# Lead of the projections and place of the x gathers in a sparse graph attention with residual layer norm

## The chip, the cores and the metric

The kernel runs on one core of one Trainium2 chip. The metric is the device time of one execution in microseconds. The chip runs the work on separate engines, each with its own queue of instructions: PE multiplies matrices, DVE does vector arithmetic, ACT computes activations and copies, POOL (GpSimd) issues the indirect DMAs and does a few small operations, and SP issues most of the plain DMAs.

## The reference

For 16 batches of 1024 nodes with 512 features, eight heads of 64:

```python
q = (x @ Wq + bq).reshape(b, n, H, HD)
k = (x @ Wk + bk).reshape(b, n, H, HD)
v = (x @ Wv + bv).reshape(b, n, H, HD)
scores = einsum('bqhd,bkhd->bhqk', q, k) / sqrt(HD)
scores = scores + (1.0 - adj)[None, None, :, :] * -1000000000.0
attn = softmax(scores, axis=-1)
out = einsum('bhqk,bkhd->bqhd', attn, v).reshape(b, n, d)
x = layernorm(x + out @ Wo + bo)
```

One adjacency matrix serves all batches. It is sparse, and the first rows have far more neighbours than the last ones: an edge between nodes i and j has a probability that falls with the square roots of both.

## The kernel before, in words

The kernel does not multiply with the full adjacency. It sorts the 1024 queries by their number of neighbours, cuts them into eight tiles of 128 (t = 0 to 7), and looks up for each query the list of its keys. All further work goes by *blocks*: a block (b, t, i) takes, for the 128 queries of tile t in batch b, one key per query. Own blocks take the i-th key of each query of the tile; deep blocks (BLOCKS, tiles 6 and 7) take further keys of the queries that have many, and a matmul with a 0/1 matrix (`sums`) adds their results to the right queries. The list of all blocks has 530 entries, 32 or 34 a batch, and `start[b]` is the first of batch b: 430 for batch 13, 464 for 14, 496 for 15.

For one block, POOL gathers 128 rows of keys and values (`kvg`, L1242) from DRAM, DVE multiplies them with the queries (`qk`, L1263) and sums by head (`s`, L1267), ACT takes the exponential (L1278), ACT or DVE weighs the values (`pv`, L1291 and L1295), and DVE adds them (L1307) or PE adds them for deep blocks (L1316, L1317). At a tile's end DVE divides by the sum (`o`, L1337), PE transposes the result (`poT`, L1351), ACT copies it (`oT`), and `finish` has PE multiply it with Wo (`po`, L790). `complete` then adds the residual x and normalises: DVE (L1099, L1100), ACT (squares, L1107), POOL (the power, L1113 and L1143), ACT (L1121) and a POOL scatter to the output (L1125).

Before its blocks a batch needs its projections. These are the *fronts*: a list of PE units for all batches in order. For a pair of tiles they hold the transposition of x (`pxT`, L748), the products for q (`pq`, L790), and seven products that give k and v of two tiles by a Strassen scheme (`x`, `pp`, `z`, L947). The results of each are written to DRAM (`q_rows`, `kv_pair`) by SP, and the blocks gather from there. Two batches from batch 2 on form a pair: they share a table `kv_pair`, tile 0 of the even batch is served in the odd one, and at an odd batch's start POOL also gathers `more` (L1217) from the pair's table.

The order of everything is written by a loop over places n = -39 to 541, one place for each block, at build time. At place n the program issues the kvg gather of block n + 8 (n + 11 when the fronts have run out), the products and scores of block n + 4, the exponential of n + 3, the weighting of n + 1 or n + 2, the addition of n, and the delayed steps that earlier places planned: `later(k, fn)` runs fn k places later. PE's place in this order goes by credit: each place adds a `share` of PE time, and units of the fronts or of finishing tiles are issued until the credit is used up. The planner counts 0.86 us for a product, 0.44 for a transposition and 0.87 for a sum. At each batch's start the share is set so that the fronts still to come meet a goal:

```python
ahead = EARLY + FIRST * (1 - max(0, b - 1) / LATE)
goal = fronts_time - needed(b + 2, ahead / NBT)
```

`ahead` is thus the lead in places: how much of batch b + 2 is to be done when batch b ends. From batch 13 on (LATE + 1) the share is set so that the fronts run out at `fronts_end`. When fronts and tiles compete, a finished tile waits in `done`; some tiles (`SPILL`, 20 of them) are stored to DRAM meanwhile and are reloaded and finished only after the fronts have run out, up to one a second place.

x comes in tiles of 128 rows into three buffers. `load_x(b, t)` takes a buffer and, from batch 1 on, has POOL gather the rows (L1001). It is called from `out`, the step one place behind the transposition of an earlier tile, for the tile three further on: there ACT copies the transposed tile (`xT`), for tile 0 it also squares the rows of x (`sq_x`, L762), and for tiles in `STORED` SP writes x to DRAM (`residual`, L764), to be read again as the residual. A gather into a buffer waits until what still reads that buffer has finished; the buffers are given out in the order of the calls, the one released first first.

Of the kernel before, what the change touches and what calls it, by code (L numbers as in the profile page):

```python
# [38 lines left out]
PAIRED_FROM, SPARED = 2, 56  # L39
# [9 lines left out]
AHEAD_LAST = 11  # L49

ROWS = 3
EARLY = 13

FIRST = 11
LEAD_IN = 39
FRONT_BY = -14
SEGMENT = 64
# [120 lines left out]
def kernel(  # L178
# [37 lines left out]
    B, N, D = x.shape  # L216
    HD = D // HEADS
    NPAIR = D // P
    NT = N // P
# [34 lines left out]
    with ExitStack() as main:  # L254
# [6 lines left out]
        def fill_psum(name):  # L261
            return psum.tile([P, HALF], F32, tag="fill", name=name, bufs=4)
# [74 lines left out]
        def merged(b):  # L337
            return b >= PAIRED_FROM and b % 2 == 1
# [103 lines left out]
        def later(k, fn):  # L442
            plan.setdefault(now[0] + k, []).append(fn)
# [288 lines left out]
        def load_x(b, t):  # L732
            if b < B:
                if b and not known:
                    waiting.append((b, t))
                    return
                X[b, t] = work.tile([P, D], F32, tag="x", name=f"x_{b}_{t}", bufs=3)
                if b:
                    gather_x(X[b, t], b, t)
                else:  # L740
                    nc.sync.dma_start(X[b, t], x[b, ds(t * P, P), :])

        def transpose_x(b, t):
            def pe():
                xs = X.pop((b, t))
                p = fill_psum(f"pxT_{b}_{t}")
                for c in range(NPAIR):
                    nc.tensor.transpose(p[:, ts(c, P)], xs[:, ts(c, P)], ident)  # L748

                def out():  # L750
                    XT[b, t] = work.tile([P, D], F32, tag="xT", name=f"xT_{b}_{t}", bufs=4)
                    nc.scalar.copy(XT[b, t], p)
                    n = b * NT + t + 3
                    if t == 0 and b >= PAIRED_FROM:
                        if not merged(b):
                            BOTH[b // 2] = work.tile([P, 2, NPAIR, P], F32, tag="place", name=f"both_{b}", bufs=1)
                        nc.scalar.copy(
                            BOTH[b // 2].rearrange("p w c (h n) -> p h c w n", h=2)[:, b % 2],
                            p.rearrange("p (c w n) -> p c w n", c=NPAIR, w=2),
                        )  # L760
                        sq = work.tile([P, D], F32, tag="ysq", name=f"sq_x_{b}", bufs=1)
                        nc.scalar.activation(sq[0:LONE, :], xs[0:LONE, :], AF.Square, accum_out=x_norm[0:LONE, b:b + 1])  # L762
                    if b * NT + t in STORED:
                        nc.sync.dma_start(residual[b * NT + t], xs)  # L764
                        later(2, lambda: load_x(n // NT, n % NT))
                    else:
                        load_x(n // NT, n % NT)
                    if t % 2 and (b, t) != (0, 1):
                        later(1, combine)

                def combine():
                    s = [work.tile([P, HD2], F32, tag=f"s{i}", name=f"s{i}_{b}_{t}", bufs=1 + i // 4) for i in (1, 2, 3, 4)]
                    x0, x1 = XT[b, t - 1], XT[b, t]
                    nc.vector.tensor_tensor(s[0], x1[:, 0:HD2], x1[:, HD2:D], op=OP.add)
                    nc.vector.tensor_tensor(s[2], x0[:, 0:HD2], x1[:, 0:HD2], op=OP.subtract)
                    nc.vector.tensor_tensor(s[1], s[0], x0[:, 0:HD2], op=OP.subtract)
                    nc.vector.tensor_tensor(s[3], x0[:, HD2:D], s[1], op=OP.subtract)
                    SX[b, t // 2] = s

                later(1, out)  # L780

            return [(TRANSPOSE, pe, lambda: (b, t) in X)]
# [217 lines left out]
        def gather_x(y, b, t):  # L1000
            nc.gpsimd.indirect_dma_start(  # L1001
                out=y, out_offset=None, in_=x_rows,
                in_offset=bass.IndirectOffsetOnAxis(ap=asked_row[:, t:t + 1], axis=0), element_offset=b * N * D,
            )
# [181 lines left out]
        start = [min(n for n, block in enumerate(blocks) if block[0] == b) for b in range(B)] + [len(blocks)]  # L1186
# [276 lines left out]
        with tc.manual_schedule():  # L1463
# [9 lines left out]
            def needed(b, part):  # L1473
                b += int(part)
                if b >= B:
                    return fronts_time
                return fronts_by[b - 1] + (part - int(part)) * (fronts_by[b] - fronts_by[b - 1])

            finishing, last_finish, reloads, last_reload = [], -LEAD_IN, 0, 0
            fronts_end = start[B - 1] - 12  # L1480
            credit = 0.0
            for t in range(3):
                load_x(0, t)
            n = -LEAD_IN
            while n < total or plan or rest or urgent or done or finishing or spilled or lone_tiles or not guarded:
# [6 lines left out]
                elif n in start:  # L1492

                    b = start.index(n)
                    left = sum(u[0] for u in fronts)
                    ahead = EARLY + FIRST * (1 - max(0, b - 1) / LATE)
                    goal = fronts_time - needed(b + 2, ahead / NBT)
# [107 lines left out]
```

## Time and profile before

| what | us |
|---|---|
| median of 3 runs | 1888.14 |
| lowest and highest | 1887.98, 1894.98 |
| the profiled execution | 1894.52 |
| its span in the profile | 1892.4 |

The profile is of one execution, and its span leaves 2.1 us of that execution's time outside. The prediction shows lines of several of its views. A line of the page's groups or of the timeline names the source line, the engine, the operation and the tiles, written `out<-in` without buffer numbers. The chain of waits goes back from the last instruction to what released it, and lists start, length, engine, tile and line; `issue` is time in which the engine waited for nothing that the profile shows. A line of the waits names who waited for whom, the total, the number of times and the longest. In the busy times by window, each engine has its busy microseconds and, in brackets, its instructions. Records of PE overlap, so that their mean duration is longer than their distance in a stream.

### The profile page before, as it was taken

The page shows a single profiled execution, that of the slowest core. Times are in us where ns is not written, and L with a number is a line of the kernel's source. Part 1 is how long each engine was busy: PE and PEld are TensorE (multiplying, and loading weights), DVE is VectorE, ACT ScalarE, POOL GpSimd, SP SyncE. Part 2 cuts the span into 40 slices and gives each one's busy share as a digit, 9 for nine tenths or more (in the row PEclk, how much of TensorE's full clock was granted, in tenths as well). Part 3 has the DMA queues.
Part 4 walks back from the last instruction along what each step waited for, and adds up shares of the span by engine and source line. Part 5 has one row for each costly group of instructions (what it writes and reads, how often), then busy time and mean ns, then how long its engine had stood idle before and what let it go on. Part 6 is the DMA issues. An engine that isn't in the chain of part 4 may idle for free. (4 is left out here: it accounts for less than half of the span.)

```text
span 1892.4 us, 25171 instructions
## 1 busy us (share of the span) xinstructions
PE 1816.5 (96%) x5149; PEld 876.6 (46%) x5149; DVE 1695.3 (90%) x3470; ACT 1557.4 (82%) x6128; POOL 1262.6 (67%) x1189
## 2 busy tenths in 40 slices
PE   7979999999999999999999999999999999999996
PEld 3434444444545454444444444444545444444442
DVE  6888879999998999899999989899999989997875
ACT  3627868988888988988898878988899989977885
POOL 1366765777676776767676766767676866656884
PEclk9989999999999999999999999999999999999998
DMA  7356786888989897989889897989889899989993
GB/s 279 115 167 215 226 290 229 309 298 291 322 266 319 303 333 256 345 290 310 299 284 329 279 324 261 334 303 309 286 302 352 297 332 319 329 282 319 340 332 137
DMA packets 188149, 544.63 MB, mean 288 GB/s; under 512 B 32602, under 2 KB 32622, under 8 KB 187986
## 3 DMA queue, kind: packets, MB, share of 16 engines
q0 software_dynamic: 116400, 382.82, 60.4%
q1 hardware_dynamic: 68510, 154.30, 21.7%
q10 hardware_dynamic: 3076, 5.82, 0.8%
q14 instruction: 120, 0.98, 0.2%
q8 instruction: 43, 0.70, 0.2%
HBM read 419.52 MB, written 144.34 MB: 298 GB/s over the span
## 5 line engine op out<-in xcount | busy, mean ns | idle before, releaser
L1291 ACT ACTIVATE pv<-kvg,pv 128x64 f32<-128x64 f32 x3544 | 893.4, 340 | 1.8 <-issue 1.8
L1242 POOL DMA_INDIRECT kvg<-kv_pair,place_row x462 | 522.6, 1131 | 258.6 <-issue 94.5
L790 PE MATMUL po<-wo,oT 128*128 128x512 f32 x816 | 379.2, 600 | 2.0 <-DVE vsum L854 1.2
L790 PE MATMUL pq<-wq,xT 128*128 128x512 f32 x792 | 369.4, 598 | 1.3 <-DVE s L1267 0.8
L1267 DVE TENSOR_REDUCE s<-qk 128x8 f32<-128x512 f32 x530 | 360.8, 681 | 7.2
L1263 DVE TENSOR_TENSOR qk<-qt,kvg 128x512 f32<-128x512 f32 x434 | 296.8, 684 | 13.2 <-DMA kvg<-kv_pair,place_row 13.1
L947 PE MATMUL x<-b,xT 128*128 128x512 f32 x504 | 239.0, 597 | 0.1
L947 PE MATMUL pp<-t,s 128*128 128x512 f32 x504 | 237.3, 593 | 1.5 <-DVE t L383 1.5
L1307 DVE TENSOR_TENSOR pv<-pv,pv 128x520 f32<-128x520 f32 x329 | 228.4, 694 | 8.2 <-ACT pv L1291 8.0
L790 PEld LDWEIGHTS po<-wo,oT 128*128 128x128 f32 x816 | 153.4, 192 | 171.7 <-issue 162.7
L790 PEld LDWEIGHTS pq<-wq,xT 128*128 128x128 f32 x792 | 149.0, 192 | 169.3 <-issue 157.7
L1001 POOL DMA_INDIRECT x<-in_x_dram,asked_row x120 | 129.6, 1080 | 103.5 <-PE pxT L748 35.4
L1278 ACT ACTIVATE pv<-s,absent 128x8 f32<-128x8 f32 x434 | 126.8, 293 | 55.1 <-DVE s L1267 36.6
L1125 POOL DMA_INDIRECT out_dram<-y,asked_row x129 | 145.1, 1125 | 35.9 <-issue 25.0
L800 ACT ACTIVATE sq_k<-kv 128x128 bf16<-128x128 f32 x512 | 150.8, 300 | 8.4 <-DVE kv L970 4.5
L947 PEld LDWEIGHTS x<-b,xT 128*128 128x128 f32 x504 | 95.3, 192 | 111.6 <-issue 105.2
L947 PEld LDWEIGHTS pp<-t,s 128*128 128x128 f32 x504 | 94.1, 190 | 111.3 <-issue 102.2
L947 PE MATMUL z<-b,s 128*128 128x512 f32 x252 | 121.4, 604 | 13.1 <-DVE kv L975 10.4
L1196 POOL DMA_INDIRECT qg<-q_rows,query_row x96 | 105.5, 1099 | 28.5 <-issue 25.3
L1029 POOL DMA_INDIRECT y<-in_x_dram,asked_row x93 | 105.0, 1129 | 26.1 <-issue 25.8
L947 PE MATMUL z<-t,s 128*128 128x512 f32 x252 | 118.6, 593 | 0.0
L947 PE MATMUL pp<-t,xT 128*128 128x512 f32 x252 | 118.5, 592 | 0.0
(276 smaller groups left out, 2750.2 us busy)
## 6 DMA issues: line engine op xcount, KB each, us to landing
kv_pair<-kv SPq DMA_DIRECT2D x98, 512.0 KB
q_rows<-q SPq DMA_DIRECT2D x106, 256.0 KB
qt<-q_rows SPq DMA_DIRECT2D x98, 256.0 KB
residual<-x SPq DMA_DIRECT2D x36, 256.0 KB
y<-residual SPq DMA_DIRECT2D x36, 256.0 KB
kv_rows<-kv SPq DMA_DIRECT2D x15, 512.0 KB
kvg<-kv_pair,place_row POOLq DMA_INDIRECT x462
kv_pair<-kv SPq DMA_DIRECT2D x28, 256.0 KB
```

The source lines that it names most:

```text
L790: nc.tensor.matmul(p, lhs(c), w[:, c, :], start=(c == 0), stop=(c == NPAIR - 1))
L800: nc.scalar.activation(sq, s[:, ts(h, P)], AF.Square, scale=scale, accum_out=sums[:, h:h + 1])
L947: nc.tensor.matmul(R[bank], l[:, ts(c, P)], right[:, c, :], start=(first and c == 0), stop=(c == 1), skip_group_check=True,)
L1001: nc.gpsimd.indirect_dma_start(out=y, out_offset=None, in_=x_rows, in_offset=bass.IndirectOffsetOnAxis(ap=asked_row[:, t:t + 1], axis=0), ...
L1125: nc.gpsimd.indirect_dma_start(out=out_rows[b, t], out_offset=bass.IndirectOffsetOnAxis(ap=rows, axis=0), in_=y, in_offset=None, element_o ...
L1196: nc.gpsimd.indirect_dma_start(out=q, out_offset=None, in_=q_rows[b % ROWS], in_offset=bass.IndirectOffsetOnAxis(ap=rows, axis=0))
L1242: nc.gpsimd.indirect_dma_start(out=KG[n], out_offset=None, in_=rows, in_offset=bass.IndirectOffsetOnAxis(ap=(place_row if b else key_row)[ ...
L1263: nc.vector.tensor_tensor(QK[n], q, KG[n][:, 0:D], op=OP.mult)
L1267: nc.vector.tensor_reduce(S[n], QK.pop(n).rearrange("p (h d) -> p h d", d=HD), axis=AX.X, op=OP.add)
L1278: nc.scalar.activation(PV[n][:, D:], S.pop(n), AF.Exp, bias=bias)
L1291: nc.scalar.activation(pv[:, ts(h, HD)], v[:, ds(D + h * HD, HD)], AF.Copy, scale=pv[:, D + h:D + h + 1])
L1307: nc.vector.tensor_tensor(PV[b, t], PV[b, t], pv, op=OP.add)
```

## The change

Three things are changed. EARLY goes from 13 to 17 and FIRST from 11 to 7, so that `ahead` is 24 places for the first batches in both kernels and 17 in place of 13 at the end. `fronts_end` goes from 12 places ahead of the last batch's start to 16. And the x gather that `out` calls comes later in two cases: behind a tile that is stored as residual four places later in place of two, and behind tile 0 from batch 2 on, where x is squared, two places later in place of at once.

```diff
-EARLY = 13
+EARLY = 17
 
-FIRST = 11
+FIRST = 7
...
                     if b * NT + t in STORED:
                         nc.sync.dma_start(residual[b * NT + t], xs)
+                        later(4, lambda: load_x(n // NT, n % NT))
+                    elif t == 0 and b >= PAIRED_FROM:
                         later(2, lambda: load_x(n // NT, n % NT))
                     else:
                         load_x(n // NT, n % NT)
...
-            fronts_end = start[B - 1] - 12
+            fronts_end = start[B - 1] - 16
```

## The prediction

> **What bounds the kernel now.** I read the page's busy times first, then the chain of waits of the last 260 us, then busy times by stage, then the waits of single engines. First the page:
>
> ```profile
> span 1892.4 us, 25171 instructions
> PE 1816.5 (96%) x5149; PEld 876.6 (46%) x5149; DVE 1695.3 (90%) x3470; ACT 1557.4 (82%) x6128; POOL 1262.6 (67%) x1189
> ```
>
> PE leads, with DVE close behind. The chain shows what a matmul really costs:
>
> ```profile
> 1677.35 3.43 PE po L790 x8
> 1680.79 1.72 PE pq L790 x4
> ```
>
> Eight records (four matmuls, one tile's output projection) take 3.43 us end to end, 0.43 a record, where the groups' mean is 600 ns: records overlap. From 1650 to 1721 us the chain holds PE pieces alone: there PE is the bound and has no gap. Summing, over the trace, each PE record's start against 0.43 us (in proportion for shorter ones), PE has gaps of 43 us in all between 384 and 1745 us, of which 10 lie in 1018 to 1124 us and 11 in 1535 to 1636 us, and none worth naming between 1636 and 1745. Columns of the next view: window, length, then busy us of PE, PEld, DVE, ACT, POOL, the granted clock, DMA share.
>
> ```profile
> 1535.00:1636.00 101.00, 93.67 (x270) 44.76 (x269) 94.44 (x181) 89.97 (x370) 66.54 (x62) 0.98 0.90 311
> 1636.00:1745.00 109.00, 107.75 (x298) 51.52 (x297) 98.33 (x198) 90.83 (x362) 65.09 (x61) 1.00 0.90 314
> 1745.00:1826.00 81.00, 78.14 (x226) 36.72 (x225) 68.06 (x190) 65.93 (x212) 66.78 (x61) 1.00 0.92 336
> 1826.00:1859.00 33.00, 31.12 (x83) 14.89 (x82) 25.79 (x65) 23.95 (x80) 23.59 (x23) 0.95 0.86 301
> 1859.00:1892.00 33.00, 16.79 (x43) 7.63 (x41) 11.37 (x45) 14.97 (x35) 14.11 (x15) 0.83 0.26 97
> ```
>
> The reader is to see a full PE up to about 1859, then an end in which nothing is full. Batch 13 begins at 1535 us, 14 at 1636, 15 at 1745 (the 430th, 464th and 496th qk product on DVE; place n's product is issued at place n-4). The last place's product starts at 1858.5. Its end is held by PE: the chain runs through output projections of older tiles, and DVE queues behind them.
>
> ```profile
> 1858.70 3.43 PE po L790 x8
> 1862.35 1.72 PE po L790 x4
> 1864.94 1.72 PE po L790 x4
> 1866.87 1.73 PE po L790 x4
> 1869.33 0.63 DVE pv L1307
> ```
>
> The waits from 1826 us on say the same of DVE (total, times, longest):
>
> ```profile
> DVE y L1100 <- PE po L790: 9.0, 4, 4.2
> ```
>
> Last, POOL between 384 and 1640 us, where the moved gathers stand:
>
> ```profile
> POOL x L1001 <- PE pxT L748: 19.2, 10, 4.3
> POOL x L1001 <- ACT sq_x L762: 10.3, 5, 3.5
> POOL x L1001 <- DMA residual<-x: 7.9, 3, 6.0
> POOL more L1217 <- issue: 6.4, 6, 4.9
> ```
>
> **The skill beside the trace.** The Trainium skill, TensorE: Matmul & The Clock Gate, section "Back-to-back issue gap" and the steps before it, says that matmuls keep program order and that a stream of them costs its columns, since drain and fill overlap. The trace agrees: 0.43 us a record in a stream against 600 ns for one. So I count 0.43, and a PE instruction moved earlier costs its full time there unless PE had a gap. DMA: Bandwidth & Descriptors, section "Anatomy of one DMA", says that a DMA's semaphore wait is served on the issuing sequencer before dispatch. The rows above agree: POOL, not a DMA engine, sat up to 6.0 us before an x gather, with the kvg gathers of later places behind it. The forecast goes by both.
>
> **Part 1, the lead.** EARLY + FIRST is 24 in both, so the first batches keep their lead; it falls to 17 places at the end in place of 13. The fronts now end at start[B-1] - 16. I followed the planner's own credits for both kernels; its units (0.86, 0.44, 0.87 us) are the trace's (3.43 / 4, 0.44, 0.87). The front units run out at place 481, not 485. No work is added or removed but one bias matmul (0.22 us) and one DVE addition (0.6 us). So this is a move. Set beside the products, PE work changes by stage as: places 68 to 430 +6.9 us, batch 13 +0.8, batch 14 +3.5 (14 output projections in place of 11), places 496 to 520 +3.7, and behind 520 -14.6: 6 output projections in place of 10, four of 3.43 + 0.22 us.
>
> Behind 520 (1826.4 us to the end, 66 us). Nine places take 32 us, of which DVE is busy 25.8 with four y rows that go away (4 x 0.75 us). At 22.8 us DVE would be the next bound; ACT and POOL stand at 24 and 23.6 and lose four square, normalise, store and load steps as well (0.8 + 0.8 us on ACT, about 2 on POOL). I take 26 us for the nine places: -6. Then the last place: its product starts at 1858.5 and its weighted value is added at 1869.3, 10.8 us later, with DVE waits for po of 2.28 and 2.35 us between and a PE backlog until 1868. Without older projections I estimate 4.8 us (product 0.69, sum 0.68, exponential 0.3, weighting and addition 0.69 each, semaphores between): -6. The remaining 23 us from there to the end are the last tile's own and stay. Together -12, bounds -4 (ACT and POOL hold the rhythm) and -14.6.
>
> Places 496 to 520 hold PE gaps of some 2 us: +3. Batch 14 is PE's without a gap: +3.5. Places 68 to 430: +6.9 falls in part into the 31 us of gaps there, but those are mostly waits for DVE, whose load moves along; I take +4.5, bounds 0 and +6.9. Batch 13 has 11 us of gaps: +0.8 costs nothing.
>
> **What the lead frees.** At the start of batch 13 POOL stands 4.95 us before it can gather, because the pair's last rows are only being written (timeline: start, length, engine, line; in brackets the idle time before it):
>
> ```profile
> 1526.75 1.96 POOL L1217 DMA_INDIRECT more<-kv_pair,place_row  x1 [4.95 <-issue]
> 1538.72 0.69 DVE L1263 TENSOR_TENSOR qk<-qt,kvg 128x512 f32<-128x512 f32 x1 [1.47 <-DMA kvg<-kv_pair,place_row]
> 1543.34 0.69 DVE L1263 TENSOR_TENSOR qk<-qt,kvg 128x512 f32<-128x512 f32 x1 [1.53 <-DMA kvg<-kv_pair,place_row]
> ```
>
> DVE then waits 3.4 us for kvg in three rows and 2.2 us for POOL. Four places are some 12 us, over twice the wait, so it goes: -4 (0 to -5.6). What is late next there is DVE, 94 of 101 us. At the start of batch 14 DVE waits 1.57 and 0.91 us for kvg: -1.5.
>
> **Part 2, the x gathers.** No DMA is added. Of the 120 gathers those behind a kept x go from 2 to 4 places later, those behind a squared x from 0 to 2, so that x tile 3 is asked for after tile 4 and takes the other's buffer. POOL's waits for squares (10.3 us) and for residual stores (7.9 us) go, and some of the 19.2 us for pxT. POOL is 70% busy there, and its kvg waits are mostly for a buffer that ACT or DVE still reads, so little of this was on the path: I take -1 (0 to -4). SP's queue keeps its order but for what the lead moves. The price is a later x. A gather is issued about four places behind its emission, and PE is as late, so the distance is gap x 3.1 us. From batch 2 on the smallest gap was 4, three times; now fourteen are 3 or 4, and x(14,5) has 1, some 3 to 5 us. The chain shows an x landing in 3.25 us and kvg in 3.8 to 8.6 us; x(14,5) itself was used 6.6 us after issue without a stall. I price +2 there (0 to +4), and nothing for gaps of 3 (9.3 us).
>
> **Sum.** -12 + 3 + 3.5 + 4.5 - 4 - 1.5 - 1 + 2 = -5.5; the four freed DMA-heavy finishes also lighten a DMA share of 0.86 to 0.92 in the end, so I round to -6. Against the profiled execution's own 1894.52 us (span 1892.4 and 2.1 around it) that is 1888.5; the profile ran 6.4 us over the median of the runs, 1888.14, and the same saving gives 1882.
>
> **Rivals.** (a) The end is not PE's: places 520 to 529 keep their 3.2 us, because ACT, POOL and DVE hand each other the work (the chain from 1819 to 1849 us runs through these three). Then the end saves only 4 us while everything before pays its 14.9 in full and nothing is freed: +11, 1899, slower. It decides once the end saves less than the earlier stages pay, about 7 us. Against it: 19 us of the chain behind 1849 are PE's. (b) The lead removes jitter too: PE's gaps of 43 us shrink by a quarter, the added work is all absorbed: -16, 1872. For it: at 1097.8 us PE waits 4 us for a DVE that had been held up. Against: DVE is over 90% busy in most stages. (c) Work is only moved and the end's gain is paid back exactly, or the gathers come late again: 1888.
>
> **How the numbers follow.** About half a percent, 9.4 us, is what a measurement of this kernel tells from no change. Forecast 0.50 (own range 1876 to 1889), (b) 0.20, (c) 0.14, (a) 0.16. Below 1878.7: all of (b) and a third of the forecast, 0.36; above 1897.6: most of (a), 0.13; the rest 0.51. The range reaches to both rivals: 1870 to 1898.
>
> **What would show it.** After: the last place's product at about 1850 us and DVE's addition some 5 us behind it; no po of stored tiles in the chain behind it; the wait of POOL for more gone at batch 13; POOL's waits for sq_x and residual gone; batch 14 no shorter; PE idle before pxT of x(14,5) at most 4 us. It is wrong if batches 2 to 12 grow by more than 7 us, if x comes late in several places, or if the rhythm behind 520 stays at 3.2 us.

## The result, and the profile after

| | us |
|---|---|
| kernel before, median of 6 runs beside the changed one | 1895.13 |
| changed kernel, median of 6 runs (1912.83 to 1918.69) | 1916.08 |
| ratio, 95% interval | 1.0106 [1.0077, 1.0135] |
| forecast | 1882, range 1870 to 1898 |

The change makes the kernel 1.06% slower, about 20 us, where 6 us less were forecast. Three of the six runs of before are those of the table ahead of the prediction; the other three took 1895.28 to 1902.64, and against their median, 1899.99, the loss is 16 us. The page of the kernel after, first lines:

```profile
span 1913.5 us, 25168 instructions
PE 1824.0 (95%) x5150; PEld 880.2 (46%) x5150; DVE 1696.0 (89%) x3469; ACT 1557.1 (81%) x6128; POOL 1260.9 (66%) x1189
```

No engine got more to do: DVE, ACT and POOL are busy for the same time as before within 2 us, and PE's 7.5 us more are hardly work either (its instructions are the same but for one bias product), as will be seen. The time went into waiting. Where it went, the stages tell. The busy times by window of the kernel after (window, length, then busy us of PE, PEld, DVE, ACT, POOL with their instructions, granted clock, DMA share, GB/s); the windows are places 68 to 430, batch 13, batch 14, places 496 to 520, 520 to 529, and the rest:

```profile
383.90:1559.90 1176.00, 1143.34 (x3266) 556.01 (x3265) 1083.18 (x2118) 1017.83 (x4114) 800.09 (x743) 0.99 0.87 300
1559.90:1658.60 98.70, 94.48 (x269) 45.37 (x268) 95.05 (x182) 91.05 (x375) 68.54 (x61) 0.98 0.90 316
1658.60:1770.40 111.80, 111.80 (x310) 53.45 (x310) 95.04 (x199) 87.72 (x345) 66.40 (x63) 1.00 0.91 327
1770.40:1850.40 80.00, 79.27 (x228) 37.55 (x227) 70.31 (x195) 71.35 (x233) 66.13 (x58) 1.00 0.87 308
1850.40:1882.80 32.40, 26.53 (x69) 12.69 (x67) 23.48 (x62) 21.96 (x69) 24.98 (x24) 0.95 0.80 273
1882.80:1913.50 30.70, 10.97 (x21) 5.03 (x21) 10.72 (x36) 11.53 (x30) 11.24 (x12) 0.59 0.19 70
```

The first row of the kernel before, whose length was not shown ahead:

```profile
384.40:1535.20 1150.80, 1131.51 (x3245) 551.05 (x3244) 1078.77 (x2110) 1015.79 (x4106) 802.45 (x740) 1.00 0.88 304
```

Against the terms of the forecast (batch 13 and the rest of before by the same places: 1535.2, 1635.9, 1745.3, 1826.4 and 1858.5 us to the end at 1892.4):

| stage | before | after | change | forecast |
|---|---|---|---|---|
| places 68 to 430 | 1150.8 | 1176.0 | +25.2 | +4.5 (0 to +6.9) |
| batch 13 | 100.7 | 98.7 | -2.0 | -4 |
| batch 14 with its start | 109.4 | 111.8 | +2.4 | +3.5 - 1.5 |
| places 496 to 520 | 81.1 | 80.0 | -1.1 | +3 |
| places 520 to 529 | 32.1 | 32.4 | +0.3 | -6 |
| place 529 to the end | 33.9 | 30.7 | -3.2 | -6 |

With -0.5 us ahead of place 68 the column gives the 21.1 us between the spans. So two terms failed: the middle, by some 20 us, and the end, by 9. The others together are within 4 us.

**The end.** The nine places last as long as before, though PE is busy for only 26.53 us of them and DVE for 23.48. The POOL part of the timeline (start, length, engine, line; in brackets the idle time ahead of it) shows that POOL has less room than its busy time says:

```profile
1855.05 1.43 POOL L1198 DMA_INDIRECT qg<-q_rows,query_row  x1 [0.31 <-issue]
1856.79 1.01 POOL L1244 DMA_INDIRECT kvg<-kv_pair,place_row  x1 [0.30 <-DMA kvg<-kv_pair,place_row]
1858.10 1.23 POOL L1127 DMA_INDIRECT out_dram<-y,asked_row  x1 [0.30 <-ACT y L1123]
1859.63 1.02 POOL L1244 DMA_INDIRECT kvg<-kv_pair,place_row  x1 [0.30 <-issue]
1860.69 0.72 POOL L1145 TENSOR_TENSOR stats<-stats,neg_half 128x2 f32<-128x2 f32 x1
```

No two of these DMAs follow each other closer than 0.30 us. Counting with each POOL instruction the idle time behind it, where that is at most 0.35 us, fills all of the 81.1 us of places 496 to 520 before and 79.6 of the 80.0 after, at a busy share of 83% (66.13 of 80.00). In places 520 to 529 it fills 27.5 of 32.1 us before and 30.0 of 32.3 after: much, but not all. DVE waits for POOL there, as the waits from 1850 us of after say, and those of 1826.4 to 1858.5 us of before:

```profile
DVE stats L1118 <- POOL stats L1115: 4.9, 2, 4.2
```

```profile
DVE stats L1116 <- POOL stats L1113: 4.2, 1, 4.2
```

The wait of 4.2 us falls into the nine places in both kernels. The experiments below show what this says of the bound, and what not.

**The middle.** PE's work can be set apart from its waiting with the 0.43 us a record of the prediction; what a record takes longer than that counts as idle time. Before to after, the work in places 68 to 430 is 1119.8 and 1126.2 us (+6.4, close to the 6.9 that the forecast counted), PE's idle time 30.9 and 49.3 (+18.4). Most of this growth, 13 us, is in long single stalls: four of over 1.4 us before, 10.0 us together, and nine of 23.0 after. Some of the larger waits of PE and DVE there, after:

```profile
PE z L949 <- DVE kv L977: 12.3, 6, 4.3
DVE y L1101 <- ACT out_mean L1050: 5.9, 5, 2.1
DVE s L776 <- PE z L949: 5.1, 2, 3.1
PE sum L1318 <- ACT pv L1293: 3.1, 1, 3.1
```

Before:

```profile
PE z L947 <- DVE kv L975: 9.2, 4, 3.9
DVE y L1099 <- ACT out_mean L1048: 0.5, 1, 0.5
```

Before has no row of s behind z. The reader is to see that no one wait grew by 18 us. There are more of them, of PE for DVE and of DVE for PE and ACT. How one comes about is seen at place 390, in PE's and DVE's rows of the timeline of after:

```profile
1423.64 1.88 PE L949 MATMUL z<-t,s 128*128 128x512 f32 x4
1425.36 1.88 PE L949 MATMUL pp<-t,xT 128*128 128x512 f32 x4
1425.63 0.42 DVE L776 TENSOR_TENSOR s<-xT 128x256 f32<-128x256 f32 x1 [2.00 <-PE z L949]
...
1427.13 0.68 DVE L1265 TENSOR_TENSOR qk<-qt,kvg 128x512 f32<-128x512 f32 x1
...
1427.73 0.69 DVE L1309 TENSOR_TENSOR pv<-pv,pv 128x520 f32<-128x520 f32 x1
...
1430.26 0.69 DVE L977 TENSOR_TENSOR kv<-z,g 128x512 f32<-128x512 f32 x1
...
1431.01 3.67 PE L949 MATMUL z<-b,s 128*128 128x512 f32 x4 [3.77 <-DVE kv L977]
```

DVE stands 2.00 us before the next pair's sums, because PE is still reading the old sums for z (the tile `s1` has one buffer). Behind that stand some 4.6 us of DVE work, and only then comes `kv<-z,g`, which empties z's bank. PE comes to the second z of the pair with nothing in between but one unit `pp`, and stands 3.77 us. PE was late for DVE, and then DVE for PE.

And the stall costs more than its length: the four records behind it take 3.67 us, where the same four take 1.88 above. The windows ahead of the stall, of the stall and behind it have the granted clock in the third column from the right:

```profile
1420.00:1427.30 7.30, 7.13 (x16) 2.96 (x16) 3.74 (x10) 7.30 (x40) 4.50 (x5) 1.00 0.76 272
1427.30:1431.00 3.70, 0.00 (x0) 0.00 (x0) 3.67 (x8) 3.70 (x19) 2.64 (x3) 1.00 0.69 209
1431.00:1434.50 3.50, 3.49 (x5) 1.44 (x6) 3.43 (x9) 3.50 (x16) 2.39 (x3) 0.52 0.71 205
```

After 3.7 us without a matmul the clock is 0.52 for the next 3.5 us. The Trainium skill, TensorE: Matmul & The Clock Gate, section "What's actually happening", says that the array falls to half rate after an idle window of about 3.4 us and needs a busy one to come back. This stall is that long; other stalls here were shorter and had the same effect (last section), so 3.4 us of unbroken idle time are not needed. PE's busy time counts these slow records at their length, and the last record ahead of a stall at its full 0.6 us, which is why PE seems to have more to do.

### The profile page after: what moved, and what is told of

It is laid out like the page before. It is cut to its first block, busy times and chain, and to the rows that moved or that the text cites. A ratio compares the mean times of both kernels' runs of the same rounds, so it can differ in the third digit from the quotient of the medians.

```text
span 1913.5 us, 25168 instructions
## 1 busy us (share of the span) xinstructions
PE 1824.0 (95%) x5150; PEld 880.2 (46%) x5150; DVE 1696.0 (89%) x3469; ACT 1557.1 (81%) x6128; POOL 1260.9 (66%) x1189
## 3 DMA queue, kind: packets, MB, share of 16 engines
q1 hardware_dynamic: 68510, 154.30, 21.4%
## 5 line engine op out<-in xcount | busy, mean ns | idle before, releaser
L1293 ACT ACTIVATE pv<-kvg,pv 128x64 f32<-128x64 f32 x3544 | 894.0, 342 | 0.3
L1003 POOL DMA_INDIRECT x<-in_x_dram,asked_row x120 | 133.2, 1110 | 81.6 <-PE pxT L748 29.4
L1127 POOL DMA_INDIRECT out_dram<-y,asked_row x129 | 150.7, 1168 | 37.0 <-issue 23.9
```

Source lines behind the costliest of these rows:

```text
L1003: nc.gpsimd.indirect_dma_start(out=y, out_offset=None, in_=x_rows, in_offset=bass.IndirectOffsetOnAxis(ap=asked_row[:, t:t + 1], axis=0), ...
L1127: nc.gpsimd.indirect_dma_start(out=out_rows[b, t], out_offset=bass.IndirectOffsetOnAxis(ap=rows, axis=0), in_=y, in_offset=None, element_o ...
L1293: nc.scalar.activation(pv[:, ts(h, HD)], v[:, ds(D + h * HD, HD)], AF.Copy, scale=pv[:, D + h:D + h + 1])
```

## The experiments

Five theories were set against each other (in the recorded expectations TensorE is PE, VectorE is DVE and ScalarE is ACT). P: POOL sets the last batch. L: the lead costs on PE in proportion to the work that it moves into places 68 to 430. X: the later x gathers cost. J: each order of PE's work has its own stalls at single places, so that parts of the change don't add. A: ACT's queue is what is late. Ratios are to the kernel before on the same chip, with 95% intervals. Chips differ (the kernel before ran 1877 to 1911 us on those used here), so traces are compared within one chip.

### The parts alone

```diff
-EARLY = 13
+EARLY = 17
-FIRST = 11
+FIRST = 7
```

> EARLY 17 and FIRST 7 alone; the x gathers and fronts_end as before. Whole change: +20 us (ratio 1.0106). Theory L (the earlier projections push PE work into stages that DVE and ACT already fill, and the end gives nothing back): this run carries most of it, +10 to +20 us, growing between places 130 and 430. Theory X (the later x gathers, with tile 3 asked for after tile 4, are what hurts): within 3 us of the kernel before. Theory J (neither has a cost of its own; each shift of PE's place against DVE and ACT re-rolls which of them waits): any size from -10 to +20, and the parts don't add up.

```diff
-            fronts_end = start[B - 1] - 12
+            fronts_end = start[B - 1] - 16
```

> fronts_end 16 places ahead of the last batch in place of 12, alone. Nothing changes before place 430. Theory L and my forecast's tail: behind place 520 fewer output projections; if the end is PE's, -4 to -8 us; if ACT, POOL and DVE hold its rhythm (my rival a), 0 to +4 us with the time from place 520 to the end still 63 to 66 us. Theory X: 0.

The third kernel has the two later x gathers of the change's diff alone:

> The two later x gathers alone (4 places behind a kept x, 2 behind a squared x); lead and fronts_end as before. Theory X: +12 to +20 us, with PE idle ahead of pxT or of the first product of a pair. Theory L: -3 to +2 us, with POOL's waits for sq_x and residual gone. Theory J: anything from -10 to +15.

The fourth has the lead and the end of the fronts, and the x gathers as before:

> The whole change without the later x gathers. Theory L: +15 to +20 us, as the whole change. Theory X: -8 to +3 us. Theory J: not the sum of the lead alone and the end alone, by 5 us or more.

| edit | ratio |
|---|---|
| lead alone | 1.0104 [1.0073, 1.0136] |
| end of the fronts alone | 1.0025 [1.0010, 1.0041] |
| later x alone | 1.0061 [1.0032, 1.0089] |
| lead and end | 1.0097 [1.0059, 1.0135] |
| all three | 1.0106 [1.0077, 1.0135] |

The three parts alone would add to +1.9%, and together they make +1.06%: they don't add. The lead by itself makes the whole loss (+21.4 us, just above what L and J had). The end alone lost 5.1 us: its expectation had -4 to -8 if the end is PE's, and 0 to +4, with 63 to 66 us from place 520 on, if it is not; those places took 63.3 us. The later x alone lost 12.5 us, at the lower edge of X and within J. The kernel with the end alone has the same order as before up to place 430, so on one chip it is the control for the lead. Its row and that of the lead for places 68 to 430:

```profile
392.30:1549.80 1157.50, 1132.81 (x3238) 550.80 (x3243) 1078.44 (x2111) 1017.86 (x4106) 799.37 (x740) 1.00 0.88 302
```

```profile
394.80:1576.30 1181.50, 1148.14 (x3257) 556.70 (x3261) 1083.52 (x2117) 1017.19 (x4113) 799.88 (x744) 0.99 0.87 297
```

+24.0 us, of which +6.3 are PE's work (1118.0 to 1124.3 by 0.43 us a record) and +17.7 its idle time (39.0 to 56.7). Both profiles are of executions above the median of their kernel, that of the lead of the slowest of its six (1934.62 us, median 1927.20), so these sizes may be somewhat high. The lead's own stalls again bring slow records: the eight of an output projection, 3.43 us in the prediction, take 6.54 behind a stall of 3.59. Timeline of PE with the lead alone:

```profile
1430.52 6.54 PE L790 MATMUL po<-wo,oT 128*128 128x512 f32 x8 [3.59 <-issue]
```

With later x alone, PE, DVE and ACT keep their order, and yet 9.7 us are lost in these places (1157.5 to 1167.2). Two waits of PE there:

```profile
PE pxT L748 <- ACT oT L1357: 5.0, 1, 5.0
PE pxT L748 <- DMA x<-in_x_dram,asked_row: 2.1, 1, 2.1
```

x came late once, x(13,5) at place 399, for 2.1 us. In the kernel with all three parts PE waits for no x in these places, and the x part adds nothing that can be told from zero (1.0097 against 1.0106). Theory X falls for the change as a whole.

The kept x's gather was then moved alone:

```diff
                     if b * NT + t in STORED:
                         nc.sync.dma_start(residual[b * NT + t], xs)
-                        later(2, lambda: load_x(n // NT, n % NT))
+                        later(4, lambda: load_x(n // NT, n % NT))
```

> Only the kept x's part of the two gathers that go two places later: the next x behind a kept x is asked for four places after in place of two; behind a squared x it stays as before. The two parts together gave +0.61%. By the wait for x(13,5) at place 399 (2.2 us, behind a kept x) this part carries most of it: +0.3 to +0.6%. If the squares' part carries it (x gathered behind sq_x, two places later in every second batch): within 0.15%.

1.0000 [0.9990, 1.0010]: a miss. By what is left, the 0.6% of both belong to the squared x's gather, to the two together, or to the chip, for the two were run on different ones; the squared part was not run alone, so this stays open.

### How much lead

Three more leads, with EARLY + FIRST kept at 24: EARLY 15 and 16, between before and the change, and 11, less than before.

> EARLY 15, FIRST 9: half of the lead's step, nothing else. Theory L (loss in proportion to the PE work that is moved into places 68 to 430): +8 to +12 us. Theory J (each order has its own stalls between PE, DVE and ACT at single places, and they don't follow the amount): not half; from -5 to +25 us, with steps at places other than those of the whole lead.

> The kernel before with EARLY 16 and FIRST 8, one step short of the change's 17 and 7. Measured leads: 11 gave +0.92%, 13 is before, 15 +0.15%, 17 +1.04%. If the loss grows smoothly behind 15 (theory L with a threshold), 16 gives +0.4 to +0.8%, with TensorE's stalls at the places of 17 (153, 244, 388, 390), shorter. If every lead has its own order and its own stalls (theory J), it can give anything from -0.2 to +1.2%, and its stalls over 1.4 us stand at other places.

> EARLY 11, FIRST 13: a shorter lead of the late batches, two places the other way. Theory L: -8 to -12 us in places 68 to 430, less what the end then has to do. Theory J: slower as well, +3 to +20 us, since the order before is one that was free of long stalls.

| EARLY | 11 | 13 | 15 | 16 | 17 |
|---|---|---|---|---|---|
| ratio | 1.0092 | 1 | 1.0015 | 1.0094 | 1.0104 |
| interval | 1.0062 to 1.0121 | | 0.9986 to 1.0044 | 1.0077 to 1.0111 | 1.0073 to 1.0136 |

(11 and 15 ran on one chip, 16 and 17 on two others.) L as a proportion falls: 15 costs almost nothing, 16 nearly all, and less lead than before costs as much as more. The kernel with the kept x alone, at 1.0000, ran on the chip of 16 and so is its control there. Their rows for places 68 to 430:

```profile
375.70:1516.50 1140.80, 1126.27 (x3232) 549.77 (x3236) 1079.02 (x2111) 1013.28 (x4101) 800.24 (x739) 1.00 0.89 306
```

```profile
375.20:1534.00 1158.80, 1135.93 (x3250) 554.66 (x3254) 1080.56 (x2113) 1012.63 (x4100) 815.26 (x743) 0.99 0.88 303
```

Of these +18.0 us, 4.7 are PE's work and 13.3 its idle time (24.7 to 38.0). So on a second chip, too, the idle time grew by more than the work. A selection of PE's stalls (us of idle time of PE at a place, read from each trace's PE rows; values under 0.6 are left out, and every kernel has others):

| place, what waits | before | 15 | 16 | 17 (lead alone) | changed kernel |
|---|---|---|---|---|---|
| 153 z | 1.23 | 0.98 | 2.06 | 4.13 | 4.26 |
| 244 poT | | | 1.92 | 1.92 | 1.92 |
| 220, 221 z | 2.67 | 2.06 | 4.03 | 1.13 | 1.06 |
| 290 z | 3.86 | | | | |
| 324 z | | 7.72 | | | |
| 388 po | | | | 3.59 | 1.48 |
| 390, 391 z | | 1.53 | 1.42 | 3.75 | 3.77 |
| 423 z | | | 2.24 | 2.66 | 2.06 |

Two of these stalls belong to the order with their length: the one at 290 is 3.84 to 3.86 us in six kernels with the lead of before (before itself, the end alone, x alone, kept x alone, ScalarE lighter, POOL's scatters moved to SP) and in none with another lead; that at 390 is 3.74 to 3.77 in five with EARLY 17. Others keep their place but not their length: the one at 388 is 3.59 us with the lead alone, 1.48 in the changed kernel and under 0.6 in the changed order with ScalarE lighter. This is what J says. It is no proof that nothing grows with the lead: 16 and 17 share the stalls at 153, 244 and 423, and the expectation for J at 16, stalls at other places, came only in part.

### POOL in the last batch

Here the tiles finished after the fronts have run out are stored by SP, a plain DMA into a scratch tensor in place of POOL's scatter; these rows are missing from the output.

```diff
             def store():
+                if not fronts:
+                    left = dram.tile([P, D], F32, name=f"left_{b}_{t}")
+                    nc.sync.dma_start(left[0:n, :], y)
+                    del Y[b, t]
+                    return
                 nc.gpsimd.indirect_dma_start(
```

> The kernel before, but tiles that are finished after the fronts have run out are stored by SP into a scratch tensor in place of POOL's scatter (the output rows of these tiles, those of about the last two batches and the stored tiles, are left out; the bytes moved are the same). Theory P: from place 496 to 520 POOL has no idle time beyond the 0.3 us between its instructions, so POOL, not PE, sets the last batch. Then places 496 to 520 shrink from 81 us to PE's work, about 76, and the whole by 6 to 12 us. If PE holds the end (my forecast): within 3 us of the kernel before.

> The changed kernel with the same scatters taken off POOL (same rows left out). Theory P: the end at last gives back what the lead moved away: from place 520 to the end 8 to 12 us less than in the kernel before with its scatters off POOL, and 10 to 18 us less than the changed kernel as a whole. If PE or DVE's own work holds the end: from place 520 to the end the same 63 us as in the changed kernel.

Before with it: 0.9929 [0.9899, 0.9959]; the changed kernel with it: 1.0049 [1.0021, 1.0077]. Windows of before with it, places 520 to 529 and the rest:

```profile
1842.40:1870.30 27.90, 27.80 (x76) 13.62 (x77) 25.10 (x65) 22.89 (x76) 8.23 (x10) 1.00 0.73 266
1870.30:1897.80 27.50, 15.99 (x45) 7.45 (x43) 11.80 (x47) 15.41 (x37) 2.20 (x4) 0.93 0.39 139
```

The changed kernel with it:

```profile
1870.60:1897.90 27.30, 24.67 (x68) 11.72 (x67) 23.41 (x62) 21.46 (x69) 8.40 (x9) 1.00 0.67 241
1897.90:1922.70 24.80, 11.17 (x21) 5.23 (x21) 10.79 (x37) 11.56 (x30) 2.98 (x4) 0.65 0.24 87
```

Behind place 520 the time falls from 66.0 to 55.4 us before and from 63.1 to 52.1 after, 11 us in both; the nine places give 4.2 and 5.1 of that, the last place and what follows it 6.4 and 5.9. So for the nine places P holds: with POOL out of the way they are shorter, and in before PE is full there (27.80 of 27.90). That the DMA share falls too is part of the edit, so POOL's queue and its DMAs' load are not told apart. POOL is not the only holder, either: with VectorE lighter (the experiment after this one), and POOL's work as it was, the nine places of before's order take

```profile
1787.70:1816.10 28.40, 26.16 (x71) 12.50 (x72) 19.93 (x63) 19.87 (x65) 21.30 (x23) 1.00 0.94 344
```

28.4 us, where the same order with ScalarE lighter takes 32.2 on the same chip. In before the nine places thus hang on POOL and DVE, which wait for one another; in the changed kernel a lighter VectorE gives little (31.6 us). The gain that I had looked for, an end some 8 to 12 us shorter in the changed kernel, is 3.3 us even with POOL free. And for places 496 to 520 P fails: they did not become shorter (84.3 and 84.2 us), and the kernel with the end alone, where POOL with its gaps fills only 75.8 us of them, takes 81.6. The changed kernel stays 1.2% behind before when both have the free POOL (1.0049 / 0.9929): the end would not have paid for the lead.

### Lighter queues on VectorE and ScalarE

If the idle time is two nearly full queues waiting for one another, lighter queues should take it away. Each edit was made in the kernel before and in the changed one. VectorE lighter:

```diff
-            QK[n] = work.tile([P, D], F32, tag="qk", name=f"qk_{n}", bufs=2)
-            nc.vector.tensor_tensor(QK[n], q, KG[n][:, 0:D], op=OP.mult)
+            QK[n] = work.tile([P, D // 2], F32, tag="qk", name=f"qk_{n}", bufs=2)
+            nc.vector.tensor_tensor(QK[n], q[:, 0:D // 2], KG[n][:, 0:D // 2], op=OP.mult)
...
-            nc.vector.tensor_reduce(S[n], QK.pop(n).rearrange("p (h d) -> p h d", d=HD), axis=AX.X, op=OP.add)
+            nc.vector.tensor_reduce(S[n], QK.pop(n).rearrange("p (h d) -> p h d", d=HD // 2), axis=AX.X, op=OP.add)
```

> The kernel before with each place's product of query and key, and its sum into scores, made over 256 of the 512 columns (half of each is left out; nothing else moves). By the rows of s<-xT (128x256: 421 ns against 684) VectorE gives back 2 x 0.26 = 0.52 us a place, 188 us in places 68 to 430, where it was idle only 79. It is the control for a_dve. If the waits between TensorE and VectorE came of VectorE's queue being nearly full (theory J), TensorE's idle time there falls from 39 us to 10 to 25, and the whole to 0.98 to 0.99 of before. If TensorE's idle comes of its own order alone (theory L), the time stays within 0.5% of before.

> The changed kernel with the same halves left out. What tells the theories apart is its time less that of b_dve, which the full kernels have at +20 us. Theory J (with the lead, TensorE's order stands worse against VectorE's nearly full queue, and each waits for the other): with room on VectorE the excess in places 68 to 430 falls from 24 us to the 6 us of TensorE's added work, and the whole is 0 to +8 us against b_dve. Theory L (the lead costs on TensorE, whatever VectorE has to do): +16 to +24. Theory A (it is ScalarE's queue that is late): also +16 to +24, as ScalarE keeps its work.

ScalarE lighter:

```diff
-                for h in range(HEADS):
+                for h in range(0, HEADS, 2):
                     nc.scalar.activation(
-                        pv[:, ts(h, HD)], v[:, ds(D + h * HD, HD)], AF.Copy, scale=pv[:, D + h:D + h + 1]
+                        pv[:, ds(h * HD, 2 * HD)], v[:, ds(D + h * HD, 2 * HD)], AF.Copy, scale=pv[:, D + h:D + h + 1]
                     )
```

> The kernel before with ScalarE's weighing of v in four copies of 128 columns in place of eight of 64 (two heads take one weight, so the weights of every other head are left out). 1772 of its 3544 copies of 340 ns go; a wider one costs somewhat more (120 columns more in the 128x512 copies of 576 ns would be 0.04 us), so about 500 us of ScalarE's 1557 go. It is the control for a_act. ScalarE was no bound of before: theory J with VectorE as the partner expects 0.99 to 1.00 of before; theory A 0.98 to 0.99, with TensorE's idle time in places 68 to 430 down from 39 us by more than 10.

> The changed kernel with the same. Against b_act, theory A (ScalarE's queue is what turns the shifted order into waits) expects 0 to +8 us, with the excess of places 68 to 430 down from 24 to about 6; theory J with VectorE as the partner, and theory L, +14 to +24.

Both at once:

> The kernel before with both lightenings at once: VectorE's products of query and key over half of the columns, ScalarE's weighing in four copies of 128 columns in place of eight of 64 (half of the products and every other head's weights are left out). The control for a_both. If TensorE's idle time in places 68 to 430 (38.9 us on one chip in the full kernel, 11.7 with VectorE alone lightened) is waits on the two engines' queues, under 6 us are left, and the whole is 0.97 to 0.985 of before.

> The changed kernel with both. Its excess over b_both in places 68 to 430 was 24 us full, 17 with VectorE lightened (7 of work, 10 of idle time), 20 with ScalarE lightened. Theory J (the two queues together turn the shifted order into waits): the idle part falls to 0 to 4 us, so that 7 to 11 us are left there, all TensorE's added work, and the whole is +5 to +12 us against b_both. Theory L (the idle part comes of TensorE's order alone): 16 to 18 us stay there, 10 of them idle, and the whole stays at +13 to +17.

Ratios to the kernel before, and places 68 to 430 in us. All six lighter kernels ran on one chip. The first row is the kernel before and the changed one; the second, for these places only, the end alone and the lead alone, both on another chip (their whole times do not compare, as they differ in the end too):

| pair | before's order | changed order | difference of medians | length | PE work | PE idle |
|---|---|---|---|---|---|---|
| full, before and changed | 1 | 1.0106 [1.0077, 1.0135] | 20.9 | +25.2 | +6.4 | 30.9 to 49.3 |
| full, end alone and lead alone | | | | +24.0 | +6.3 | 39.0 to 56.7 |
| ScalarE lighter | 0.9978 [0.9971, 0.9985] | 1.0076 [1.0056, 1.0096] | 16.7 | +20.6 | +7.1 | 19.6 to 32.6 |
| VectorE lighter | 0.9871 [0.9854, 0.9887] | 0.9945 [0.9928, 0.9961] | 14.2 | +17.7 | +7.0 | 11.7 to 22.0 |
| both | 0.9824 [0.9802, 0.9846] | 0.9904 [0.9886, 0.9922] | 15.6 | +15.3 | +7.9 | 8.9 to 16.0 |

Lighter queues do take PE's idle time away: on this one chip it falls in the order of before from 19.6 us with ScalarE lighter to 8.9 with both (J had under 6), and a lighter VectorE makes the order of before 1.3% faster, as J had it and L had not. The full rows are of other chips, and the order of before idled 24.7 us on one chip and 39.0 on another, so a fall from them can be the chip's. The decisive number did not come out as J had it: the changed order stays 14 to 17 us slower, where J asked for at most 8 with VectorE lighter and 12 with both. That is hardly less than the full pair's 20.9 us, whose interval reaches down to 14.6. L's +13 to +17 for the whole with both did come; its 16 to 18 us in these places, 10 of them idle, were 15.3 and 7.1. Theory A, ScalarE's queue alone, falls: with it lightened (by 306 us, not the 500 expected) the difference is 16.7 us. With both lightened six stalls of over 0.4 us are left in the changed kernel, 8.1 us together, against one of 3.3 in the order of before. The longest is at place 390 again:

```profile
1387.39 3.46 PE L949 MATMUL z<-b,s 128*128 128x512 f32 x4 [3.21 <-DVE kv L977]
```

The stalls at 388 and 299 (1.48 and 2.25 us in the changed kernel) are gone and that at 153 is 0.97 us, but at 390 PE waits 3.21 us with VectorE 17% less busy (903 us in these places, against 1083): kv still stands behind the sums, a product, and the additions of DVE's order. So there seem to be two kinds of stall: those that go with a lighter queue, and those that stay with the written order. In the kernel before, the stall at 290 is of the second kind (3.31 us with both lightened).

The pair with both lightened also shows the plain account of the change. PE's work before place 520 grows by 7.9 + 3.9 + 0.9 = 12.7 us (places 68 to 430, 430 to 496, 496 to 520), and behind it shrinks by 12.5. The former cannot cost less than its length where PE is full; the latter gives back 63.0 - 61.4 = 1.6 us.

### More work between the two z products

One line is moved, so that two transpositions of the next pair stand between the two z:

```diff
-            units += xt
             units += unit("z", s(1), T1, True, out_v1, None)
             units += q1
             units += unit("p4", lambda: a(1, 1), T4, True, out_k1, None)
+            units += xt
```

> The kernel before with one line moved: the transposes of the next pair's x (two units, 0.86 us each at 0.43 us a 512-column matmul) stand between the two z products of a pair in place of ahead of the first, so that TensorE has more to do while VectorE takes v1 out of z's only bank. PE's waits z<-DVE kv in places 68 to 430 are 9.2 us in before, and the slow matmuls behind them some 2.5 more. Theory J (single stalls at such joints are what an order costs): these waits fall to under 3 us; -4 to -12 us, unless x then waits for its own copies of xT, which would show as x<-ACT xT at 58 pairs x 0.2 to 0.5 us (+12 to +29).

> The changed kernel with the same line moved. Its waits z<-DVE kv are 12.3 us in places 68 to 430 (4.3 at place 153, 3.8 at 390, 2.1 at 423), with 7 or so matmuls at half the rate behind them. Theory J: these stalls go, and a_xt is -8 to -16 us against the changed kernel, at +4 to +12 us of before. Theory L: the loss does not depend on these joints, and stays at +16 to +20 of b_xt.

Before with it: 1.0352 [1.0327, 1.0377]; changed with it: 1.0391 [1.0363, 1.0419]. PE's waits there, before with the line moved:

```profile
PE pp L947 <- DVE s L776: 33.7, 18, 4.8
PE x L947 <- ACT xT L752: 6.3, 3, 4.2
PE z L947 <- DVE kv L975: 2.1, 2, 1.1
```

The wait for kv went from 9.2 to 2.1 us as expected, and a larger one took its place, on DVE's sums of the next pair, not on ACT's copies as I had guessed. In size both expectations were missed by far: the two kernels are 68 and 73 us slower than before. They differ by 4.6 us, not 20, so L's +16 to +20 did not come; but PE idles at other joints all along in them, and that is consistent with J and shows little more.

## Why the prediction was wrong

**The term for places 68 to 430, +4.5 with bounds 0 and +6.9, is the step that failed most: it measured +24 to +25.** Its count of moved work was right (6.9 us counted, 6.3 to 6.4 measured). Wrong was the upper bound, which took PE's idle time as a cover that could only shrink. It grew by 18 us. "Mostly waits for DVE, whose load moves along" stood in the prediction, and was the reason to look closer: with PE, DVE and ACT each running a fixed order, moving PE's work against the other two makes new joints. In the runs, 6 to 8 us of the loss are PE's work and about 18 are idle time, most of it in new stalls at single places. With both queues light the idle part is 7 us; how much of the other 11 is due to the queues, and how much to the chip and the execution, is not shown, since the whole loss hardly fell (20.9 to 15.6 us). Why the planner's order has its stalls just there, and whether a different lead of 17 places without them exists, was not tried.

**The term for the end, -12, was the second: it measured -3.** It took PE as the bound of the nine places and DVE as the next, by their busy shares, and put POOL at 23.6 us of 33. POOL's 0.3 us behind each DMA were left out, and so were the waits of POOL and DVE for one another; PE's 4 us less of work there shortened nothing. This is rival (a), in which ACT, POOL and DVE hand each other the work: its "the end saves only 4" is what came, and its +11 is too small mainly by the idle time of the middle. Of the last place's own -6, the addition of the weighted value comes 6.6 us behind the product (1889.4 against 1882.8) where it was 10.8, and no output projection of a stored tile stands behind the last product any more: this part went as described. It gave 3.2 us, not 6, because 6.6 us are more than the 4.8 estimated and because the last tile's own output projection, after a PE that had idled, ran at half clock for longer (its eight records take 6.24 us, 5.40 in before).

**The x gathers, -1 and +2:** POOL's waits for sq_x are gone, those for residual stores stay. Waits of POOL from 384 to 1665 us after:

```profile
POOL x L1003 <- PE pxT L748: 11.0, 8, 3.1
POOL x L1003 <- DMA residual<-x: 7.2, 3, 2.7
POOL more L1219 <- issue: 1.6, 6, 0.3
```

POOL's time ahead of them went into waits for kvg's buffers instead (ACT pv L1291 47.0 us before, L1293 65.9 after), so nothing was gained. Alone, the x part costs 0.6%, which no step foresaw; in the changed kernel no loss of its own can be seen, nor a wait of PE for x(14,5).

**Right were** the wait for `more` (longest 4.9 us, now 0.3): PE's idle time in batch 13 fell by the 4 us of the forecast, but its work grew by 2 us in place of 0.8, so that the batch became 2.0 us shorter; batch 14 no shorter, +2.4 against +2; and 0.43 us a record as PE's price while its clock is full. Places 496 to 520 got 0.7 us more of PE's work, not 3.7, and lost 2.0 us of its idle time; POOL with its gaps was full there in both kernels, but as its relief did not shorten them, what sets their length is left open.

The prediction named three signs of being wrong. Two of them came: batches 2 to 12 grew by more than 7 us, and the rhythm behind 520 stayed (32.1 and 32.4 us for nine places, which is 3.6 us a place and not the 3.2 that the prediction wrote). The third, x late in several places, did not.

## What to carry to other kernels

Moving work from one engine's late stage to its early ones pays only if that engine has slack early and is the bound late. Both are to be read from the stage itself, and an engine's fixed gap behind each instruction belongs to its load. But even an engine that is full by this count was not shown to be the bound until its relief shortened the stage. Where several engines run in an order written at build time, idle time of the bounding engine is not to be counted as a reserve for added work: here, shifting its order against the others' gave it new stalls at single places, one of which the traces of five kernels show at the same place and length. So a change of lead is to be measured at several values; the neighbours of a good one (11 and 16 beside 13 and 15) cost 0.9%.

## What the runs showed of the hardware

- Behind many stalls of PE, matmul records came at 0.86 us in place of 0.43, at half the granted clock, for 3.4 us or twice that. The stall need not be long: with the lead alone half clock came behind one of 1.92 us (timeline, and the window behind it), and not behind one of 1.75 us. Places 68 to 430 hold 9 such records with the end alone and 23 with the lead alone: 14 x 0.43 = 6 us of the 17.7 between them.

```profile
971.62 0.74 PE L1351 MATMUL poT<-ident,o 128*128 128x128 f32 x4 [1.92 <-DVE y L1099]
```

```profile
972.07:975.48 3.41, 3.41 (x6) 1.44 (x5) 2.64 (x6) 3.41 (x14) 2.50 (x4) 0.50 0.79 260
```

- POOL leaves 0.30 us between two indirect DMAs that are issued back to back, beside 1.0 to 1.4 us for each. The Trainium skill, GPSIMD Engine Reference, section "Instruction dispatch", gives one indirect call of tens of cycles for each instruction, on the path of an addition; it has no figure for an indirect DMA, and no run here shows what the 0.30 us are made of.
- The same order of work had quite different idle time on different chips: PE idled 39.0 us in places 68 to 430 on one chip (end alone) and 24.7 on another (kept x alone, at a ratio of 1.0000), with the kernel before at 1905.77 and 1877.05 us.
